# Softmax division of a latent attention by 32x32 squares, a range test on two engines, and two MLP chunks transposed on TensorE

## The chip, the cores and the metric

The kernel runs on one core of one Trainium2 chip. A core has five engines that run their own instruction streams: TensorE (PE, with its weight loads shown apart as PEld), VectorE (DVE), ScalarE (ACT), GpSimd (POOL) and SyncE (SP), which here only issues DMAs. They meet through semaphores. The metric is the device time of one execution in microseconds (us); less is better. Everything is float32.

## The reference

The input is x of 8 batches x 1024 tokens x 256. Two layers are added to it, each on a layer norm of its input:

```
x = x + latent_attention(layernorm(x))
x = x + local_transformer(layernorm(x))

latent_attention(x):                      # 16 heads of 16, rotary part of 32, causal over 1024
    c = x @ W_kv_down                     # 128 wide
    k, v, q = c @ W_k_up, c @ W_v_up, x @ W_q
    k_rope, q_rope = rotary(c @ W_k_rope), rotary(x @ W_q_rope)   # one for all heads
    s = (q . k + q_rope . k_rope) / sqrt(48)
    return (softmax(causal(s)) @ v) @ W_o

local_transformer(x):                     # 2 layers of
    q, k, v = split(shift_token(x) @ wqkv)      # 8 heads of 64
    q, k = xpos(l2norm(q)), xpos(l2norm(k))
    x = x + local_attention(8 q, k, v) @ wo     # windows of 128 with the window before
    h = layernorm(shift_token(x)) * g + b
    a, gate = split(h @ w1 + b1)                # 682 each
    x = x + (a * gelu(gate)) @ w2 + b2
```

## The kernel before

**Latent attention (`mla`, the first 1030 us).** The shared rotary part of the scores is taken out of the softmax as a factor: exp(a + r) = exp(a) x exp(r). `rotary(c, kb)` makes exp(r) for one block of keys kb and one half c of the queries: a matmul into a PSUM bank `psR`, an Exp on ACT into the tile `er` with a sum per row into `most` (L400), a minimum per row on DVE into `least` (L401), and on the diagonal a mask by POOL (L403). At the very end of the stage `most` and `least` are compared with 1e17 and 1e-17; a kernel for the general case runs instead where a value leaves that range. There are 12 such blocks per batch.

A batch is 36 units, one per step. In step s TensorE computes the scores of unit s (four matmuls of 32 rows each side by side, into two pairs of PSUM banks, `scores`, L422), ACT takes their exponentials (two instructions of 128x1024, L430), DVE multiplies the result of the unit before by `er` (`turned`, two instructions, L444), and TensorE multiplies the unit before that with the values (`values`, L455, into `acc`, 32 rows per head: 16 values, and the row sum that a column of ones in v gives). Then the step does what a table, `beside`, gives it: parts of the projections, of the rotary blocks, of the layer norm of the next batches (`statistics`, `normalise`), and of the output of this batch or the one before. Engine orders are written out by hand (`tc.manual_schedule`): the instructions stand on PE, DVE, ACT and POOL in the order in which the Python code makes them; SP's DMAs are ordered by a scheduler. The beside-work shares one pool of two PSUM banks (`psum1`, `bank`), and the scores have two buffers of two banks each.

When four heads (one g of four, for one half c of the queries) are done, `values` has ACT copy `acc` to the tile `oaT` (heads' values in partitions, tokens along the row). One step later `finished(c, g, oT)` divides: four TensorE transposes (`flip`, L203) put tokens into partitions of a bank `pst`, DVE takes the reciprocals of the sums (L472) and multiplies (L473) into `onat`. Later steps turn that back for the output projection: `out_turn(t)`, four transposes of 128x128 into `pso`, which ACT copies to `oT` (L78), and `out_add(t, i)` multiplies by W_o into `psx`, after which DVE adds to x (L500) and SP stores x2d. `value(g)` makes the values; DVE copies them from PSUM (L76). In the last batch, the output work is held back to the end of the stage (`held`). Groups end at steps 14, 15 (c = 1, g = 0, 1), 27, 28 (c = 1, g = 2, 3), 32, 33 (c = 0, g = 0, 1) and 1, 2 of the next batch (c = 0, g = 2, 3), counted by the step that holds their `finished`.

**Local transformer (`local`).** 16 passes (8 batches in layer 0, then 8 in layer 1) of 8 windows, one window per step, software pipelined over 11 steps, again ordered by hand. Each pass needs its input transposed, `xT`, which the generator `stream(b, l)` makes while the pass before runs. It is advanced (`ahead`) at the end of steps i = 3, 4, 5 of that pass, and at two places each, middle and end, of steps 6 and 7. Its parts: loads; in layer 0 the statistics of all 8 blocks; in layer 0 the normalisation of all 8 (L749); then for each half of the tokens the transposition. That is done by `squares`: DVE transposes 32x32 blocks of a tile into the tile `turned` (one buffer, L759), four DMAs write that to DRAM in an order which puts the blocks right (z), and further DMAs read it back as xT, eight per half.

The MLP runs by 32 chunks of 512 tokens (`mlp`): `look_at_chunk`, `norm_chunk` and `turn_chunk` for chunk k + 1 stand inside chunk k's work. `turn_chunk` uses `squares` too (turnedh, zh) and one DMA back into `d`; `scale_chunk` then applies gain and shift on ACT in place (L1034). The first matmuls of the chunk (`up`, ag, L1058) read d, the second ones (psy, L1099 and L1105) are added to x by DVE (L1111). psw (L991) is the output projection of the local attention. The pool `psum` with the tag "mm" has three banks, for pv, s, psw, ag, psy.

## Time and profile before

| What | Value |
|---|---|
| median of 3 runs | 3396.03 us (3395.36 to 3396.98) |
| profiled execution | 3395.82 us |
| its span in the trace | 3393.8 us |
| granted TensorE clock, mean | 0.991 |
| latent attention, one batch in the steady part | 123.02 us |
| one pass of layer 0, of layer 1 | 143.9 us, 142.8 us |
| PE, DVE, ACT, POOL busy share of the span | 97, 79, 49, 39% |

The profiled execution lies 0.2 us under the median. A row of the groups reads: line, engine, operation, tile written and tile read (names of the program), shapes, count | busy time, mean duration in ns | idle time of that engine just before such an instruction, and what ended it. Batch and pass lengths are distances from one to the next of the same instruction in the timeline. In the chain of waits each line is start, length and the work that filled it; x16 says that sixteen instructions are joined.

### The profile page before, as it was taken

How to read it: one execution, taken by the hardware profiler on the slowest of the kernel's cores; microseconds unless marked ns; L12 is line 12 of the kernel's file. 1: busy time of each engine (PE TensorE's matmuls, PEld its weight loads, DVE VectorE, ACT ScalarE, POOL GpSimd, SP SyncE). 2: the span in 40 equal slices, each digit the busy share in tenths (PEclk: the TensorE clock that was granted, in tenths of full speed). 3: DMA queues.
4: the chain of work that ended last, by engine and by line, in shares of the span. 5: the costliest groups of instructions: out<-in, count | busy, mean ns of one | idle time of the engine just before them, and what ended most of it. 6: DMA issues, size and time to landing. Idle time of an engine off the chain costs nothing.

```text
span 3393.8 us, 80114 instructions
## 1 busy us (share of the span) xinstructions
PE 3293.2 (97%) x34194; PEld 1797.8 (53%) x34194; DVE 2682.9 (79%) x4033; ACT 1673.3 (49%) x2046; POOL 1340.0 (39%) x1031
## 2 busy tenths in 40 slices
PE   8999999999997799999999999999999999999998
PEld 2434434443433456566555566565665556665664
DVE  6888988988896777887777887777877778777773
ACT  5777777777762244344444434444444444344441
POOL 1001000000006655555555555555555555555540
PEclk9999999999998899999999999999999999999999
DMA  1000000000032434445445344544545444454332
GB/s 62 8 20 26 8 20 26 8 20 14 14 104 84 128 103 116 120 112 139 111 116 129 109 126 131 144 122 136 133 136 133 126 118 128 128 141 125 107 106 60
DMA packets 370619, 313.87 MB, mean 92 GB/s; under 512 B 154655, under 2 KB 334286, under 8 KB 370126
## 3 DMA queue, kind: packets, MB, share of 16 engines
q1 hardware_dynamic: 368270, 306.26, 33.0%
q8 instruction: 271, 4.44, 0.6%
q10 hardware_dynamic: 1984, 2.41, 0.2%
q14 instruction: 94, 0.77, 0.1%
HBM read 167.00 MB, written 141.56 MB: 91 GB/s over the span
## 4 chain that ended last, share of the span: by engine, by line
PE 86%; DVE 7%; ACT 2%; issue 2%; DMA 1%; POOL 1%; SPq 1%; ACTq 0%; DVEq 0%
PE ag L1058 17%; PE pair L845 11%; PE sc L422 9%; PE acc L455 8%; PE psy L1099 7%; PE psw L991 6%; PE o L958 6%; PE pv L872 6%; PE pair L917 4%; PE psR L200 2%; PE psq L200 2%; PE psx L200 2%; PE s L966 1%; PE pst L203 1%; PE psv L200 1%
## 5 line engine op out<-in xcount | busy, mean ns | idle before, releaser
L444 DVE TENSOR_TENSOR pt<-pt,er 128x1024 f32<-128x1024 f32 x576 | 676.6, 1222 | 6.7 <-ACT pt L430 5.8
L430 ACT ACTIVATE pt<-sc 128x1024 f32<-128x1024 f32 x576 | 559.6, 1024 | 231.9 <-PE sc L422 210.6
L1058 PE MATMUL ag<-d,l 128*128 128x512 f32 x1408 | 646.2, 601 | 28.3 <-ACT d L1034 17.5
L859 POOL TENSOR_TENSOR t<-t,t 128x1024 f32<-128x1024 f32 x128 | 302.4, 2363 | 850.2 <-DVE t L855 850.2
L923 ACT ACT_TABLE_LOAD x120 | 154.0, 1283 | 701.8 <-PE pair L917 701.7
L845 PE MATMUL pair<-l_qkv,xT 128*128 128x512 f32 x1024 | 466.6, 598 | 3.3 <-ACT pt L923 1.3
L1058 PEld LDWEIGHTS ag<-d,l 128*128 128x128 f32 x1408 | 262.5, 191 | 345.5 <-issue 276.1
L125 POOL TENSOR_TENSOR rn<-ss,half 128x16 f32<-128x16 f32 x128 | 373.1, 2915 | 13.7
L422 PE MATMUL sc<-q,k 32*128 32x512 f32 (+3 forms) x3072 | 346.9, 523 | 5.6 <-ACT pt L430 5.5
L845 PEld LDWEIGHTS pair<-l_qkv,xT 128*128 128x128 f32 x1024 | 192.9, 191 | 245.1 <-issue 207.4
L455 PE MATMUL acc<-pt,v 128*32 128x512 f32 (+3 forms) x3072 | 316.3, 497 | 0.4 <-DVE pt L444 0.3
L850 ACT ACTIVATE sq<-pair 128x1024 f32<-128x1024 f32 x128 | 131.1, 1024 | 334.9 <-issue 267.1
L852 DVE TENSOR_TENSOR t<-pair,l_cos 128x1024 f32<-128x1024 f32 x128 | 156.3, 1221 | 160.4 <-ACT sq L850 155.8
L1099 PE MATMUL psy<-l,hid 128*128 128x256 f32 x1280 | 281.5, 379 | 0.0
L1099 PEld LDWEIGHTS psy<-l,hid 128*128 128x128 f32 x1280 | 243.2, 190 | 46.7 <-issue 15.1
L923 ACT ACTIVATE pt<-pair 128x1024 f32<-128x1024 f32 (+1 forms) x256 | 235.0, 968 | 63.2 <-PE pair L917 61.8
L403 POOL TENSOR_SCALAR_AFFINE_SELECT er<-er 128x128 f32<-128x128 f32 x64 | 47.3, 740 | 530.3 <-DVE least L401 530.3
L1071 DVE SCALAR_TENSOR_TENSOR hid<-ag,l_b,ge 128x512 f32<-128x512 f32 x160 | 115.8, 724 | 176.9 <-ACT ge L1070 137.1
L865 POOL TENSOR_TENSOR t<-t,rn 128x1024 f32<-128x1024 f32 x128 | 248.8, 1944 | 10.0
L958 PEld LDWEIGHTS o<-pt,v 128*32 128x32 f32 x7680 | 203.0, 110 | 93.8 <-issue 84.7
L958 PE MATMUL o<-pt,v 128*32 128x128 f32 x7680 | 239.0, 276 | 7.9 <-DVE oT L975 6.6
L991 PE MATMUL psw<-l_o,oT 128*128 128x256 f32 x1024 | 240.2, 388 | 6.2 <-DVE xs L1111 6.2
(131 smaller groups left out, 4790.2 us busy)
## 6 DMA issues: line engine op xcount, KB each, us to landing
z<-turned SPq DMA_DIRECT2D x512, 128.0 KB
qkT<-z SPq DMA_DIRECT2D x128, 512.0 KB
y<-xs SPq DMA_DIRECT2D x128, 128.0 KB
h<-y SPq DMA_DIRECT2D x32, 512.0 KB
zh<-turnedh SPq DMA_DIRECT2D x128, 128.0 KB
d<-zh SPq DMA_DIRECT2D x32, 512.0 KB
zx<-turneds SPq DMA_DIRECT2D x120, 128.0 KB
xT<-zx SPq DMA_DIRECT2D x240, 64.0 KB
```

The costliest lines, as they stand in the source:

```text
L125: nc.gpsimd.tensor_tensor(out_, in_, half[:, :n], ALU.pow)
L422: nc.tensor.matmul(two[n // 2][:, n % 2, lo : lo + w], self.k[g][rows, kb * P : (kb + 1) * P], self.q[rows, g // 2, q0 : q0 + w], start=Tr ...
L430: nc.scalar.activation(pt, sc, AF.Exp, scale=SCALE)
L444: nc.vector.tensor_tensor(t, t, er.to_broadcast([P, 1024 // w, w]), ALU.mult)
L455: nc.tensor.matmul(self.acc[g][32 * n : 32 * n + 32, q0 - c * 512 :], self.v[:, kb, h * VW : h * VW + 32], pts[n // 2][:, n % 2, lo : lo + w],
L845: nc.tensor.matmul(qk[:, n].rearrange("p h d -> p (h d)"), self.left(i)[c], w["qkv"][:, c, n * INNER : (n + 1) * INNER], start=(c == 0), s ...
L859: nc.gpsimd.tensor_tensor(t1, t1, t2, ALU.add)
L923: nc.scalar.activation(pt[:, :, : n * P], flat[:, :, : n * P], AF.Exp, scale=-1.0)
L958: nc.tensor.matmul(o[32 * j : 32 * j + 32, g, a, :], vs[m][:, h * DH + a * 32 : h * DH + a * 32 + 32], pts[m][g][:, place(j), off : off + ...
L991: nc.tensor.matmul(ps[:, i, :], oT[:, c, i * P : (i + 1) * P], self.w["o"][:, c, :], start=(c == 0), stop=(c == 3),)
L1058: nc.tensor.matmul(ps.rearrange("p (s a t) -> p s a t", a=4, t=32), w["1"][:, c, i, :], d.rearrange("p (a s) c t -> p c s a t", a=4)[:, c] ...
L1099: nc.tensor.matmul(ps[:, t, :], hid[:, i, cols], w["2"][:, i, :], start=(t == i == 0), stop=False)
```

## The change

- `finished` no longer uses TensorE. DVE transposes the 32x32 squares of oaT (128x512), takes the reciprocals and multiplies, all in SBUF; two g are packed into one tile of 16 + 16 columns. `turn_back`, one step after every second `finished`, is one more DVE transpose of 128x512 and gives the left operand of `out_add` directly. `out_turn` with its TensorE transposes and ACT copies is gone. The rows of W_o are loaded in the order that the squares leave, by eight DMAs instead of one. `onat` and `oT` are three buffers of 128x512 each.
- `value`: the copy from PSUM goes from DVE to ACT.
- `rotary`: in 6 of the 12 blocks per batch the DVE minimum is replaced by a second Exp on ACT, with the opposite sign, in place in PSUM, summed per row into `inverse`, which is compared with 1e17 at the end.
- `stream`: in layer 0 the statistics of the second half are put beside the normalisation of the first, and the normalisation of the second half comes after the next advance; the squares of both halves come one advance later, at the end of steps 6 and 7 instead of their middle.
- Chunks 0 and 31 of the MLP are transposed by TensorE into a bank of the pool "mm" (eight 128x128 transposes), and ACT applies gain and shift on the way to d; no `squares`, no DMAs. The layout of d is told to `up` through a view.

```diff
-        nc.sync.dma_start(wout, W_o.rearrange("(c p) d -> p c d", p=P))
+        for e in range(2):
+            for r in range(4):
+                lo = 32 * r + HD * e
+                nc.sync.dma_start(
+                    wout[lo : lo + HD],
+                    W_o.rearrange("(m e r p) d -> e r p m d", m=2, e=2, r=4)[e, r],
+                )
...
+        inverse = wp.tile([P, B * 12], F32, name="inverse")
+        nc.gpsimd.memset(least, 1.0)
+        nc.gpsimd.memset(inverse, 1.0)
...
-                on_v(
+                on_a(
                     self.v[:, 2 * g : 2 * g + 2, : NH * VW].rearrange("p a (h d) -> p a h d", h=NH)[..., :HD],
...
                 nc.scalar.activation(er, ps[:, :w], AF.Exp, scale=SCALE, accum_out=most[:, n : n + 1])
-                nc.vector.tensor_reduce(least[:, n : n + 1], er, AX.X, ALU.min)
+                if kb in ((0, 2), (3, 4, 5, 6))[c]:
+                    nc.vector.tensor_reduce(least[:, n : n + 1], er, AX.X, ALU.min)
+                else:
+
+                    nc.scalar.activation(
+                        ps[:, :w], ps[:, :w], AF.Exp, scale=-SCALE, accum_out=inverse[:, n : n + 1]
...
             def finished(self, c, g, oT):
-                ps = bank(f"pst{self.b}_{c}_{g}").rearrange("p (i h d) -> p i h d", i=4, h=4)
-                for i in range(4):
-                    flip(ps[:, i].rearrange("p h d -> p (h d)"), oT[:, i * P : (i + 1) * P])
-                r = self.rs[:, 4 * c : 4 * c + 4, 4 * g : 4 * g + 4]
-                nc.vector.reciprocal(r, ps[:, :, :, HD])
+
+
+                nat = late.tile([P, 16, 32], F32, tag="onat", name=f"onat{self.b}_{c}_{g}", bufs=3)
+                nc.vector.transpose(nat.rearrange("p b d -> p (b d)"), oT)
+                r = self.rs[:, c, g]
+                nc.vector.reciprocal(r, nat[:, :, HD])
+                e = g % 2
+                if e == 0:
+                    self.onat[c, g // 2] = nat
                 nc.vector.tensor_tensor(
-                    self.onat[:, 4 * c : 4 * c + 4, 4 * g : 4 * g + 4, :], ps[:, :, :, :HD],
-                    r.unsqueeze(3).to_broadcast([P, 4, 4, HD]), ALU.mult,
-                )
-
-            def out_turn(self, t):
-                if t == 4:
-                    self.oTs, self.adds = {}, {}
-                elif t == 0:
-                    verdict(self.rs.rearrange("p t h -> p (t h)"), f"a{self.b}")
-                ps = bank(f"pso{self.b}_{t}").rearrange("p (i q) -> p i q", i=4)
-                for i in range(4):
-                    flat = self.onat[:, t + i // 2].rearrange("p h d -> p (h d)")
-                    flip(ps[:, i, :], flat[:, (i % 2) * P : (i % 2 + 1) * P])
-                self.oTs[t] = late.tile([P, 4, P], F32, tag="oT", name=f"oT{self.b}_{t}", bufs=2)
-                on_a(self.oTs[t], ps)
+                    self.onat[c, g // 2][:, :, HD * e : HD * e + HD], nat[:, :, :HD],
+                    r.unsqueeze(2).to_broadcast([P, 16, HD]), ALU.mult,
+                )
+
+            def turn_back(self, c, g):
+                if g % 2:
+                    t = late.tile([P, 512], F32, tag="oT", name=f"oT{self.b}_{c}_{g}", bufs=3)
+                    nc.vector.transpose(t, self.onat.pop((c, g // 2)).rearrange("p b d -> p (b d)"))
+                    self.oTs[c, g // 2] = t
+                if (c, g) == (0, 3):
+                    verdict(self.rs.rearrange("p c g b -> p (c g b)"), f"a{self.b}")
 
             def out_add(self, t, i, c=None):
 
@@ -493,9 +508,10 @@
                     self.adds[t] = bank(f"psx{self.b}_{t}").rearrange("p (i d) -> p i d", i=2)
                 ps = self.adds[t]
                 for n in range(2) if c is None else (c,):
-                    times(ps[:, i], self.oTs[t][:, 2 * i + n, :], wout[:, n, :], n == 0, n == 1)
+                    col = (t + i) % 4 * P
+                    times(ps[:, i], self.oTs[t // 4, n][:, col : col + P], wout[:, n, :], n == 0, n == 1)
                 if i == 1 and c != 0:
-                    del self.oTs[t], self.adds[t]
+                    del self.adds[t]
...
-            (5, 0, "query", 0, 0, 1), (5, -1, "out_turn", 0), (5, 1, "normalise", 0, 1),
-            (6, -1, "out_add", 0, 0), (6, -1, "out_turn", 2), (6, 1, "normalise", 1, 0),
+            (5, 0, "query", 0, 0, 1), (5, 1, "normalise", 0, 1),
+            (6, -1, "out_add", 0, 0), (6, 1, "normalise", 1, 0),
-            (30, 1, "rotary", 1, 3), (30, 0, "out_turn", 4),
+            (30, 1, "rotary", 1, 3),
-            (34, 1, "rotary", 1, 5), (34, 0, "out_turn", 6), (34, 2, "statistics", 1, 0),
+            (34, 1, "rotary", 1, 5), (34, 2, "statistics", 1, 0),
...
-                        for act, args in held[:3]:
+                        for act, args in held[:2]:
                             act(*args)
                     ended = []
                     if len(line) > 2 or b == B and line:
                         bt, unit, pts = line.pop(0)
                         ended = [(bt, e) for e in bt.values(unit, pts)]
                     if b == B and step == 0:
-                        for act, args in held[3:]:
+                        for act, args in held[2:]:
                             act(*args)
                     do(b, step)
+                    if turning:
+                        bt, e = turning.pop(0)
+                        bt.turn_back(*e)
                     if done:
                         bt, e = done.pop(0)
                         bt.finished(*e)
+                        turning.append((bt, e[:2]))
...
+        nc.vector.tensor_scalar(ok[:, 2, :], inverse, TURN, None, ALU.is_le)
...
             if l == 0:
-                found = [statistics(xs_[:, part], f"s{b}_{n}") for n, part in enumerate(parts)]
+                found = [statistics(xs_[:, parts[0]], f"s{b}_0")]
             yield
             if l == 0:
-                for part, f in zip(parts, found):
-                    normalise(xs_[:, part], f)
+                normalise(xs_[:, parts[0]], found[0])
+                found.append(statistics(xs_[:, parts[1]], f"s{b}_1"))
             yield
             xT = pxT.tile([P, 2, T + 1], F32, tag="xT", name=f"xT{b}_{l}")
             nc.gpsimd.memset(xT[:, 1, 0:1], 0.0)
             for n in range(NCH):
+                if l == 0 and n == ((l, b) == (0, 0)):
+                    normalise(xs_[:, parts[1]], found[1])
                 if (l, b) == (0, 0):
                     for c in range(2):
                         turn(xT, 1 + n * CH, xs_[:, parts[n]], f"s{b}_{l}_{n}", chunks=(c,))
                         yield xs_, xT
                     continue
+                yield xs_, xT
                 z = zxs[n]
                 squares(xs_[:, parts[n]], f"s{b}_{l}_{n}", z)
...
                yield xs_, xT
-                yield xs_, xT
...
+        ON_PE = (0, len(chunks) - 1)
+
         def turn_chunk(k):
 
-            if k < len(chunks):
+            if k < len(chunks) and k not in ON_PE:
                 n, m = chunks[k]
                 z = zhs[k % 2]
                 squares(made[n].hs.pop(m), f"h{made[n].key(m)}", z)
@@ -1029,12 +1055,25 @@
                 nc.sync.dma_start(ds[k].rearrange("p b c t -> p (b c t)"), z.rearrange("p a f -> p (a f)"))
 
         def scale_chunk(k, w):
-            if k < len(chunks):
+            if k in ON_PE:
+                n, m = chunks[k]
+                d = p2.tile([P, 2, CH], F32, tag="d", name=f"d{made[n].key(m)}")
+                t = made[n].hs.pop(m)
+                for c in range(2):
+                    ps = psum.tile([P, CH], F32, tag="mm", name=f"psth{k}_{c}")
+                    for i in range(ST):
+                        nc.tensor.transpose(ps[:, i * P : (i + 1) * P], t[:, i, c * P : (c + 1) * P], ident)
+                    nc.scalar.activation(
+                        d[:, c], ps, AF.Identity, scale=w["gain"][:, c : c + 1], bias=w["shift"][:, c : c + 1]
+                    )
+                ds[k] = d.rearrange("p c (s a t) -> p c s a t", a=4, t=32)
+            elif k < len(chunks):
                 for c in range(2):
                     nc.scalar.activation(
                         ds[k][:, :, c], ds[k][:, :, c], AF.Identity, scale=w["gain"][:, c : c + 1],
                         bias=w["shift"][:, c : c + 1],
                     )
+                ds[k] = ds[k].rearrange("p (a s) c t -> p c s a t", a=4)
 
         def mlp():
 
@@ -1057,7 +1096,7 @@
                     for c in range(2):
                         nc.tensor.matmul(
                             ps.rearrange("p (s a t) -> p s a t", a=4, t=32), w["1"][:, c, i, :],
-                            d.rearrange("p (a s) c t -> p c s a t", a=4)[:, c],
+                            d[:, c],
                             start=(c == 0), stop=(c == 1),
                         )
                     return ps
```

More of the change, by code (lines that the diff above doesn't have):

```diff
@@ L409, in start @@
                 b = self.b
-                self.onat = late.tile([P, NT, NH, HD], F32, tag="onat", name=f"onat{b}")
-                self.rs = small.tile([P, NT, NH], F32, tag="rs", name=f"rs{b}")
-                self.acc = {}
+                self.rs = small.tile([P, 2, 4, 16], F32, tag="rs", name=f"rs{b}")
+                self.acc, self.onat, self.oTs, self.adds = {}, {}, {}, {}
             def scores(self, key, parts):
@@ L576, in mla @@
         E = mybir.EngineType
-        line, done = [], []
+        line, done, turning = [], [], []
         with tc.manual_schedule(engines={E.PE, E.DVE, E.Activation, E.Pool}):
@@ L605, in mla @@
                         bt.finished(*e)
+                        turning.append((bt, e[:2]))
                     done += ended
-        ok = small.tile([P, 2, B * 12], F32, tag="okr", name="okr", bufs=1)
+        ok = small.tile([P, 3, B * 12], F32, tag="okr", name="okr", bufs=1)
         nc.vector.tensor_scalar(ok[:, 0, :], most, TURN, None, ALU.is_le)
         nc.vector.tensor_scalar(ok[:, 1, :], least, 1 / TURN, None, ALU.is_ge)
+        nc.vector.tensor_scalar(ok[:, 2, :], inverse, TURN, None, ALU.is_le)
         verdict.add(ok.rearrange("p m n -> p (m n)"), "turn")
```

## The prediction

> **What bounds the kernel now.** I read four views, in this order: busy time by engine, busy time by stretch of time, the groups of instructions with what ended the idle time before them, and the chain of waits in three places. The page and the stretches (in the stretches each pair is length, then PE, PEld, DVE, ACT, POOL busy, the granted TensorE clock, the DMA share and GB/s):
>
> ```profile
> PE 3293.2 (97%) x34194; PEld 1797.8 (53%) x34194; DVE 2682.9 (79%) x4033; ACT 1673.3 (49%) x2046; POOL 1340.0 (39%) x1031
> ```
> ```profile
> 380.00:500.00 120.00, 118.99 (x1312) 47.74 (x1308) 106.20 (x140) 88.76 (x123) 7.96 (x10) 1.00 0.06 19
> 1035.00:1100.00 65.00, 49.14 (x461) 23.72 (x459) 48.97 (x76) 17.31 (x20) 52.38 (x32) 0.87 0.31 88
> 1100.00:1300.00 200.00, 177.94 (x1998) 106.47 (x1999) 158.58 (x257) 68.80 (x75) 117.15 (x85) 0.94 0.44 114
> 1300.00:1800.00 500.00, 494.49 (x5105) 302.42 (x5104) 395.00 (x662) 205.15 (x223) 274.95 (x205) 1.00 0.44 119
> 3300.00:3394.00 94.00, 77.69 (x470) 48.96 (x468) 35.20 (x70) 13.65 (x19) 2.23 (x3) 0.94 0.22 63
> ```
>
> The average says TensorE. The stretches say: TensorE in the latent attention (99% in 380 to 500, where DVE is at 88%) and in the passes, but neither in the fill of the second stage (1035 to 1180) nor in the tail (after 3348). So each part of the change is priced in its own stretch.
>
> ```profile
> L444 DVE TENSOR_TENSOR pt<-pt,er 128x1024 f32<-128x1024 f32 x576 | 676.6, 1222 | 6.7 <-ACT pt L430 5.8
> L430 ACT ACTIVATE pt<-sc 128x1024 f32<-128x1024 f32 x576 | 559.6, 1024 | 231.9 <-PE sc L422 210.6 <-issue 10.6 <-DMA l_cos<-in_xpos_cos_dram 4.1
> L991 PE MATMUL psw<-l_o,oT 128*128 128x256 f32 x1024 | 240.2, 388 | 6.2 <-DVE xs L1111 6.2
> L885 DVE STREAM_TRANSPOSE turned<-t 128x512 f32<-128x512 f32 x256 | 165.4, 681 | 4.1 <-POOL t L865 4.0
> L203 PE MATMUL pst<-ident,oaT 128*128 128x128 f32 x256 | 42.0, 287 | 3.5 <-ACT er L400 3.4 <-ACT oaT L78 0.2
> L401 DVE TENSOR_REDUCE least<-er 128x1 f32<-128x512 f32 x48 | 32.6, 682 | 29.7 <-ACT er L400 29.7
> L473 DVE TENSOR_TENSOR onat<-pst,rs 128x256 f32<-128x256 f32 x64 | 27.2, 425 | 2.2
> L76 DVE COPY v<-psv 128x512 f32<-128x512 f32 x32 | 22.2, 692 | 18.6 <-PE psv L200 17.9
> L203 PE MATMUL pso<-ident,onat 128*128 128x128 f32 x128 | 21.1, 286 | 0.7 <-DVE onat L473 0.7
> ```
>
> TensorE's idle time here is small in every group (the last columns): its 36 steps per batch are full of its own work. But a step has a second length. In the chain of batch 3, where TensorE has least beside the attention (steps 24 to 26):
>
> ```profile
> 492.61 1.18 PE sc L422 x13
> 495.66 1.18 PE sc L422 x8
> 498.70 1.18 PE sc L422 x8
> ```
>
> These scores start 3.05 and 3.04 us apart and take 1.18, not the 1.07 of other steps: they wait for the second exponential (L430, .92 from start to start) to free their PSUM. So about 3.07 us is the floor of a step, whatever TensorE is spared. The other two places:
>
> ```profile
> 1176.07 3.20 DMA d<-zh
> 1180.16 5.97 PE ag L1058 x8
> ```
> ```profile
> 3350.99 3.88 DMA d<-zh
> 3355.76 20.77 PE ag L1058 x44
> ```
>
> The first and the last MLP chunk come late through a DMA; TensorE is idle 8.97 us before the first (from 1171.2) and 7.61 before the last (from 3348.15).
>
> **The change part by part.** The profiled execution took 3395.82 us, of which 3393.8 is the span; the median of the runs is 3396.03, so the sum is made against 3396. What the page cannot tell, 0.2% or 7 us, I count as no change. Distances "from start to start" are from the timeline; they are less than the durations because instructions of one engine overlap.
>
> *1. Division in squares, per batch.* Removed from TensorE: 12 groups of four transposes (pst 8, pso 4). A group takes .58 start to start: 12 x .58 = 7.0 us per batch. From ACT: 4 copies oT (587 ns, .50). The new DVE work has no row of its own shape; the nearest is L885, the same instruction on the same 128x512 (681 ns, .61 start to start). Eight transposes in `finished` and four in `turn_back`: 12 x .61 = 7.3 us. Reciprocal (.25) and product (.34) stay; from SBUF instead of PSUM I take them as equal (bounds: -.1 to +.2 each).
>
> What TensorE gets from it goes by step. Lengths before, and what is left after .58 is taken, but not under 3.07: steps 1, 2, 6, 32 and 33 (3.52 each) give .45 each; 5 gives .39, 14 (3.30) .23, 15 (4.01) .58, 30 (3.86) .35, 34 (3.31) .24; 27 gives .15, because its exponentials already start .4 late behind the two masked copies of k; 28 nothing, for part 2 fills its ACT. That is 4.2 of the 7.0.
>
> *2. Range test shared, values copied by ACT, per batch.* DVE loses six `least` (.47 + .19 + 3 x .60 + .19 = 2.65) and four copies v (L76, 4 x .61 = 2.43). ACT gets four copies (nearest row: L78, .50 to .59) and six exponentials with a sum (a 512 wide one 608 ns, its read of the sum 210; net .59, so 2.3 + .6 = 2.9), less the oT copies: +2.9 of some 91 in 123, and spread; each of these steps has .9 to 1.4 us of ACT left, except 28 (.20), already counted. The inverse also holds its PSUM bank .6 longer; with pst and pso gone the two banks have room.
>
> DVE's sum is +7.3 - 2.65 - 2.43 = +2.2 us on 108.9 in a batch (106.20 of 120, times 123.0): not an average limit (111 of 121). Where it falls matters. The removed work lies in steps 2, 9, 14, 15, 24, 25 and 27 to 29, the added in 1 to 3, 14 to 16, 27 to 29 and 32 to 34. A step costs DVE 2.27 for its two products (L444, 1.135 start to start). Steps 32 to 34 come to 2.27 + .6 (sum into x) + 1.2; 2.27 + .6 (least) + 1.2; 2.27 + .47 + .8 (statistics) + .6 = about 12.2 us against 3 x 3.07 = 9.2. The products may run 1.4 us later than now before `values`, two steps on, waits for them. So 1.6 to 1.9 of stall there, and in steps 1 to 3 about .6 by the same reckoning: 2.4 (0 if DVE starts these steps early; 4.5 if the new instructions cost half as much again). Net per batch -4.2 + 2.4 = -1.8, for batches 1 to 6 -11. Batch 0 and the prologue, where ACT and psR alternate and ACT gets four inverses and two copies: +2 (.5 to 4). Batch 7 is bound by DVE after 985, and the end of the stage loses a TensorE round trip of 1.5 us: +2 together. Sum of the latent attention: -7, between -22 (no stall) and +15.
>
> At this place a rule speaks against the change. The row: a 128x512 transpose on DVE has 681 ns, four 128x128 ones on TensorE .58 us. The Trainium skill, "VectorE: DVE Perf Modes", section "Rules for kernel authors", tells authors to put a 128x128 transpose on TensorE where PSUM will do as its destination, and the section "The three transpose paths" gives 311 ns for 128x128 in 32x32 blocks on VectorE (bf16). An estimate by that page would be 4 x .311 = 1.24 per transpose, 14.9 per batch, and 7.6 more of DVE time than by the row; were all of it stall, 8 x 7.6 = 61 us slower. The row has the shape and type, so the row stands.
>
> W_o in eight DMAs instead of one: SP issues them in the prologue (.45 each by the z issues, 3.2 more), wanted first in step 31; the cover is 100 us. The memsets are POOL's, idle there. The third range check, on 96 columns, lies after the stage: under .5.
>
> *3. The streams, layer 0.* In the fill, squares of the two halves of xT stand next to each other and the second waits for the first one's DMA (`turned` has one buffer): DVE idles 3.79 (to 1111.30) and 4.15 (to 1127.55). In the whole trace:
>
> ```profile
> DVE turneds L759 <- DMA z<-turned: 91.6, 26, 7.4
> ```
>
> Half a step apart, the first goes; the second largely comes back, as the eight xT transfers are queued on SP ahead of the next. I take 3 (0 to 7). In the six steady layer-0 passes DVE is busy without a gap from the statistics (1356.67) through the eight normalisations (2.63) to L1111 (1388.76), and TensorE waits 1.03 for it. Half of both, 1.3 us, moves behind L1111: the wait goes, and what is late next is unseen, so -.75 x 6 = -4.5 (-6.2 to -1). In the other passes the 91.6 is covered (TensorE has 142.2 of 144), and that squares and xT transfers go out half a step (9 us) later on DVE and SP costs nothing as long as the transfers end before the next pass's first qk, for which some 20 us are left now; without that cover up to 9 a pass.
>
> *4. Chunks 0 and 31.* Removed: turnedh (4 x .35), four DMAs zh, one d and its issue. Chunk 0: h is ready at 1170.88; after it eight transposes (2 x .58) and ACT (.69), so ag at about 1172.8 instead of 1180.16: -7.4. But DVE works through most of that gap (8.26 of 8.9), and `hid` and the sums wait for it, so not all of it lasts: I take -6 (-9 to -2). Together with 3 the fill gives -9. Chunk 31: h is ready at 3342.3, psth0 runs at 3348.1, psth1 when L1111 (3348.06 to 3348.75) has freed its bank, ACT .69 after: ag at 3350.1, -5.6 (-7 to -3).
>
> The clock: after both gaps the granted clock is half for 5 to 7 us (the first four or five ag average 1093 and 1057 ns instead of 592). The Trainium skill, "TensorE: Matmul & The Clock Gate", section "Part 1: The HAM clock gate", has the half clock begin after about 3.4 us without work; a gap of 2 us would then keep full speed and give another estimated 1 to 2 us at each. I leave it out of the sum.
>
> Sum: -7 - 9 - 4.5 - 5.6 = -26: 3370 us.
>
> **The rivals.**
> *A, DVE keeps up.* DVE ends the products .8 to 3 us early in all steps but 28, which speaks for it; 32 to 34 against. Then 4.2 per batch: 2.4 x 6 = 14 less, 3356.
> *B, the attention gives nothing.* Stalls of 4.2 per batch cancel TensorE's gain (88% DVE busy now; the added work comes in threes). With the ends' 19 and +4 for batches 0 and 7: 3381.
> *C, slower.* DVE sets the pace where heads end: if all 7.3 us of transposes come out as stall, less 4.2: +3.1 x 7 = 22, +4, less the ends: 3403. It decides from 6.3 us of stall per batch on (net 2.1 x 7 + 4 = 19). Against: the 5.1 us removed and slack of about 2 us before most steps.
> *D, the second stage's waits were hidden anyway.* DVE has 49 of 65 us in the fill, and POOL 52; if something else follows, 3 and 4 give only chunk 31 and 3 us: 3396 - 7 - 8.6 = 3380.
>
> **How the numbers follow.** Forecast 3370 (3360 to 3378) .50; A .14; B .15; D .11; C .10. The range leaves out C and the far end of A: 3351 to 3389. Faster by over 0.2% (under 3389): .50 + .14 + .13 + .09 = .86; the same .05 from the weak ends of B and D, slower .09.
>
> **What would show it.** Batch period 123.0 before: 121.2 expected, 118.8 under A, 123 under B, over 126 under C. Steps 1, 2, 6 near 3.07. "acc <- DVE pt" waits of TensorE near steps 35 and 0: absent under A. Chunk 0: TensorE idle under 3 us near 1170. Tail: 2 us between psbad and ag. The psw wait of 6.2 gone. Wrong would make it a DVE transpose much over .68 from these layouts, or ACT late in steps 24 to 30, with exponentials starting after 1.2 us.

## The result and the profile after

The changed kernel takes 3352.9 us (median of 4, 3352.46 to 3355.65) against 3395.8 for the kernel before (4 runs): a ratio of 0.9875, with a 95% interval of 0.9858 to 0.9892. The profiled execution has a span of 3350.7 us against 3393.8, 43.1 less. Where those come from is read by following the same instruction through both timelines: how much earlier does it start? The difference between two marks is what the stretch between them gave.

| Stretch, from mark to mark | predicted | measured |
|---|---|---|
| start to batch 1 of the attention | +2 | -1.4 |
| batches 1 to 6 | -11 (-1.8 each) | -6.6 (-1.10 each) |
| batch 7 to the first qk of the second stage | +2 | +2.7 |
| fill, first qk to first psy | -9 | -13.8 |
| six layer-0 passes, psy of chunk 0 to psy of chunk 12 | -4.5 | -12.3 (-2.04 each) |
| the rest of the passes, to psy of chunk 30 | 0 | -5.3 (-.94 in each layer-1 pass, +1.15 at the change of layers) |
| tail, psy of chunk 30 to the end | -5.6 | -6.4 |
| sum | -26 | -43.1 |

Two of these rows are no clear gain or loss. From batch 7 to the first qk it takes 132.8 us in the kernel before, but 136.2 in e1 (below), which leaves the code of the attention as it is; and the pass with the change of layers takes 145.7 before and 146.8 after, but 146.4 in e4, which leaves that place as it is. So the +2.7 and most of the +1.15 lie within what runs show without an edit there.

First the busy times of the whole execution and of the stretches, kernel after (columns as before: PE, PEld, DVE, ACT, POOL, granted clock, DMA share, GB/s):

```profile
PE 3272.6 (98%) x33826; PEld 1778.5 (53%) x33826; DVE 2711.0 (81%) x4042; ACT 1692.5 (51%) x2142; POOL 1340.9 (40%) x1033
```
```profile
380.00:500.00 120.00, 118.81 (x1286) 46.34 (x1282) 108.91 (x141) 92.39 (x136) 9.16 (x10) 1.00 0.06 19
...
1094.00:1285.00 191.00, 181.61 (x2009) 108.86 (x2009) 164.06 (x267) 72.32 (x79) 120.69 (x89) 0.96 0.44 116
1285.00:1780.00 495.00, 494.55 (x5105) 302.53 (x5104) 400.69 (x661) 207.09 (x224) 279.71 (x205) 1.00 0.45 121
...
3255.00:3350.00 95.00, 85.38 (x586) 55.30 (x578) 39.34 (x79) 20.16 (x25) 5.64 (x8) 0.97 0.17 52
```

VectorE has 108.91 of 120 us in the attention (before 106.20), ScalarE 92.39 (88.76). Scaled to a batch that is 1.8 and 2.9 more, where the prediction had 2.2 and 2.9. TensorE now idles .45 us in the 495 of the layer-0 passes, where it idled 5.5 in 500 (three and a half passes in each case): some 1.5 of the 2.04 us that each pass gained. Next, groups of the kernel after:

```profile
L459 DVE TENSOR_TENSOR pt<-pt,er 128x1024 f32<-128x1024 f32 x576 | 676.2, 1220 | 32.1 <-ACT pt L445 31.7
L486 DVE STREAM_TRANSPOSE onat<-oaT 128x512 f32<-128x512 f32 x64 | 44.9, 702 | 0.0
L500 DVE STREAM_TRANSPOSE oT<-onat 128x512 f32<-128x512 f32 x32 | 22.3, 698 | 0.0
L1014 PE MATMUL psw<-l_o,oT 128*128 128x256 f32 x1024 | 240.8, 389 | 0.0
```

The new DVE transposes take 702 and 698 ns; the row from which I priced them had 681. (The estimate of 1.24 us, worked out from the 311 ns that the Trainium skill, "VectorE: DVE Perf Modes", "The three transpose paths", gives for 128x128 in bf16, does not hold for these; the measurement decides.) The psw wait of 6.2 us is gone, as predicted. Of the waits of the kernel before, two that change (engine, what waits, for what: total, times, longest):

```profile
PEld acc L455 <- DVE pt L444: 40.9, 56, 1.5
PE ag L1058 <- ACT v L78: 8.8, 13, 0.7
```

and in the kernel after:

```profile
PEld acc L470 <- DVE pt L459: 105.9, 144, 2.1
DVE turneds L780 <- DMA z<-turned: 10.9, 8, 4.5
PE acc L470 <- DVE pt L459: 8.8, 23, 1.3
```

TensorE now waits for VectorE's products: a little of it shows as idle PE (8.8 us, before .3), more in the weight loads that wait (40.9 to 105.9). The wait for `turned`, 91.6 before, has all but gone, and with it a wait that I had not priced: ag behind the copy of v no longer appears at all. Chain of waits after, in batch 3, in the fill and in the tail:

```profile
516.34 2.27 DVE pt L459 x2
520.57 2.28 DVE pt L459 x2
```
```profile
1162.53 0.69 ACT d L1066
1163.27 3.70 PE ag L1097 x8
```
```profile
3312.10 0.66 PE psth L1065 x4
...
3312.88 19.08 PE ag L1097 x44
```

The products of VectorE that are issued in steps 33 and 34 of a batch are now on the chain. The first eight ag take 3.70 us instead of 5.97, and the 44 of the last chunk 19.08 instead of 20.77: TensorE idles only .48 us before the first ag and .19 before psth of the last chunk, and the clock stays at 1.00 (windows 1163 to 1176 and 3308 to 3316). This agrees with the Trainium skill ("TensorE: Matmul & The Clock Gate", "Part 1: The HAM clock gate"), which has the half clock begin after about 3.4 us without work.

### The profile page after: what moved, and what is told of

It is laid out like the page before. It is cut to its first block, busy times and chain, and to the rows that moved or that the text cites. A ratio compares the mean times of both kernels' runs of the same rounds, so it can differ in the third digit from the quotient of the medians.

```text
span 3350.7 us, 79434 instructions
## 1 busy us (share of the span) xinstructions
PE 3272.6 (98%) x33826; PEld 1778.5 (53%) x33826; DVE 2711.0 (81%) x4042; ACT 1692.5 (51%) x2142; POOL 1340.9 (40%) x1033
## 4 chain that ended last, share of the span: by engine, by line
PE 88%; DVE 5%; ACT 2%; issue 1%; DMA 1%; SPq 1%; POOL 1%; ACTq 0%; DVEq 0%
PE ag L1097 17%; PE pair L868 13%; PE sc L437 9%; PE psy L1138 8%; PE acc L470 7%; PE psw L1014 7%; PE o L981 6%; PE pv L895 6%; PE pair L940 4%; DVE pt L459 2%; PE psx L200 2%; PE psq L200 2%; PE s L989 2%; PE psR L200 1%; PE psy L1144 1%
## 5 line engine op out<-in xcount | busy, mean ns | idle before, releaser
L437 PE MATMUL sc<-q,k 32*128 32x512 f32 (+3 forms) x3072 | 368.9, 522 | 6.5 <-ACT pt L445 6.4
L470 PE MATMUL acc<-pt,v 128*32 128x512 f32 (+3 forms) x3072 | 336.1, 497 | 9.1 <-DVE pt L459 8.8
L437 PEld LDWEIGHTS sc<-q,k 32*128 32x128 f32 x3072 | 157.9, 184 | 199.6 <-ACT pt L445 149.3
```

The lines of the kernel that those rows point to most:

```text
L437: nc.tensor.matmul(two[n // 2][:, n % 2, lo : lo + w], self.k[g][rows, kb * P : (kb + 1) * P], self.q[rows, g // 2, q0 : q0 + w], start=Tr ...
L470: nc.tensor.matmul(self.acc[g][32 * n : 32 * n + 32, q0 - c * 512 :], self.v[:, kb, h * VW : h * VW + 32], pts[n // 2][:, n % 2, lo : lo + w],
```

## Experiments

Two theories stand for the second stage. S: the wait of VectorE for the one tile `turned` cost TensorE .9 us in every pass, through what was queued behind it. H, my prediction: that wait was covered. For the attention, M: VectorE's new work stalls TensorE in the steps where heads end; and later W: the stall comes from a wait at the head of VectorE's queue, with other work behind it. Against them stand "VectorE keeps up" (A, as in the prediction) and "VectorE's amount of work counts" (B here, another than the B of the prediction).

### The streams alone, both edits, and the squares alone

```diff
  e1_streams: the two hunks of `stream` from the change
  e2_squares_later: only
+                yield xs_, xT
                 z = zxs[n]
                 squares(xs_[:, parts[n]], f"s{b}_{l}_{n}", z)
...
-                yield xs_, xT
```

> The kernel before with both edits of the streams alone (squares half a step later, statistics and normalisation spread). Theory S: in every pass DVE stood behind the squares' wait for the one tile `turned`, so the reciprocal of the sums and hid came late, a bank came free late and TensorE lost .9 us (the ag wait of .68); in layer 0 the psw wait of 1.03 goes as well. Then a layer-0 pass takes 141.9 instead of 143.9 us, a layer-1 pass 141.9 instead of 142.8, the transition gives about 1 back and the fill 1 to 4: 3374 to 3378 us. Rival H, the prediction's view (the waits were covered, only the psw wait goes): layer-0 passes 143.1, layer-1 passes unchanged at 142.8, 3388 us.

> The kernel before with the squares half a step later and nothing else. Theory S: layer-1 passes 141.9, layer-0 passes 142.9 (the psw wait of 6.2 us in all stays), the ag wait behind the copy of v is gone, total wait of DVE for z falls from 91.6 to under 20: 3379 to 3383 us. Rival H2, the spreading of the statistics is what made room: layer-0 passes stay at 143.9, only layer 1 can gain: 3389 us or more.

Measured: e1 3376.66 us, ratio 0.9946 (0.9929 to 0.9963); e2 3381.24, ratio 0.9957 (0.9940 to 0.9973). A layer-0 pass took 143.9 before, 141.9 in e1, 143.0 in e2; a layer-1 pass 142.8, 141.9, 141.9. So the squares' place gives .94 in every pass of both layers, and the spreading of the normalisation the other 1.1 in layer 0 (in e2 the psw wait of 6.2 us is still there). S holds, H falls. The fill of e1 is 2.9 us shorter from the first qk to the first psy, but its first qk came 3.4 later, so e1 does not show a gain in the fill.

### What the wait did, and taking it away without moving anything

The same place of a layer-1 pass in the timeline, before: VectorE, then TensorE (start, length, what, idle before and its end):

```profile
2415.20 1.42 DVE L759 STREAM_TRANSPOSE turneds<-xs 128x256 f32<-128x256 f32 x4 [4.04 <-DMA z<-turned]
2416.55 1.72 DVE L970 RECIPROCAL rs<-s 128x256 f32<-128x256 f32 x1
...
2419.39 0.74 DVE L1071 SCALAR_TENSOR_TENSOR hid<-ag,l_b,ge 128x512 f32<-128x512 f32 x1
```
```profile
2421.47 2.84 PE L1058 MATMUL ag<-d,l 128*128 128x512 f32 x6 [0.68 <-ACT v L78]
```

and after:

```profile
2379.87 1.74 DVE L993 RECIPROCAL rs<-s 128x256 f32<-128x256 f32 x1
...
2385.66 0.75 DVE L1110 SCALAR_TENSOR_TENSOR hid<-ag,l_b,ge 128x512 f32<-128x512 f32 x1 [2.86 <-ACT ge L1109]
2386.36 1.43 DVE L780 STREAM_TRANSPOSE turneds<-xs 128x256 f32<-128x256 f32 x4
```
```profile
2389.41 3.60 PE L1097 MATMUL ag<-d,l 128*128 128x512 f32 x8
```

Before, the squares stood at the head of VectorE's queue for 4.04 us until the DMAs had read `turned`, which the transposes of q and k had just filled. The reciprocal that frees the bank of s, and hid, which frees the banks of ag, waited behind it; by this reading the three banks of the pool "mm" ran out, and ag started .68 late. The profile names the copy of v, because that came last. After, the reciprocal runs first and the squares find `turned` free. To tell the wait from the place:

```diff
-                squares(xs_[:, parts[n]], f"s{b}_{l}_{n}", z)
+                squares(xs_[:, parts[n]], f"s{b}_{l}_{n}", z, "turned" if l else "x2")
```

(`squares` takes the tile's tag as a new argument; in layer 0 the tile of load_x2 is not in use.)

> The kernel before with its engine orders unchanged, only that in layer 0 the squares of the streams use another tile than the one that the transposes of q and k use (the tile of load_x2, which layer 0 does not need). That takes away what makes them wait, not their place. Theory S (the wait is the cause): layer-0 passes 142.9 instead of 143.9, layer 1 as before (142.8), ag waits behind v in layer 1 alone, fill 1 to 7 us shorter: 3383 to 3389 us. Rival H3 (their place is the cause: 1.4 us of transposes ahead of the reciprocal): layer-0 passes stay at 143.9, 3392 to 3396 us.

Measured: 3388.95 us, ratio 0.9976 (0.9966 to 0.9986). Layer-0 passes 143.0, layer-1 passes unchanged. The waits of e3:

```profile
DVE turneds L759 <- DMA z<-turned: 41.1, 13, 7.7
PE psw L991 <- DVE xs L1111: 6.1, 6, 1.0
PE ag L1058 <- ACT v L78: 4.7, 7, 0.7
```

With the orders of PE, DVE, ACT and POOL as before, another tile alone gives the .94 in the six layer-0 passes, which have it, and of the 13 waits of ag the 6 in layer 0 are gone: there the single buffer is the cause, not the place of the squares. For layer 1, which kept the one tile, e2 shows the same gain from the later place. The fill gave 1.2 us, at the low end of what was expected.

### The two chunks alone

The hunks of `turn_chunk`, `scale_chunk` and `up` on the kernel before.

> The kernel before with chunks 0 and 31 on TensorE and nothing else. If the saved half clock counts in full: first ag at 1172 to 1173 instead of 1180.16 and 2.3 us less after it, tail 7.9 shorter: 3378 to 3380 us. Rival, the prediction's terms (DVE holds back part of the fill, half clock left out): 6 and 5.6 us: 3384 us.

Measured: 3381.05 us, ratio 0.9953 (0.9937 to 0.9970). The fill gave 9.4 (first qk to first psy), the tail 7.7; 1.3 us were lost before chunk 30, where ag waited 2.2 us for its d. That wait is .9 in the kernel before and 2.0 in e6, whose second stage is that of the kernel before, so it moves from run to run without this edit; it puts e4 just above the 3378 to 3380 us that were expected. The chain of e4 in the tail shows the full speed:

```profile
3342.52 0.66 PE psth L1042 x4
...
3343.30 19.08 PE ag L1074 x44
```

So the saved half clock has to be counted: from the first qk, the first ag came 7.1 us earlier, close to the 7.4 of the direct path, and the eight ag took 2.3 less, together the 9.4. VectorE held back next to nothing of it.

### The attention: division alone, sharing alone

```diff
  e5_division: the change's `finished`, `turn_back`, `out_add`, W_o; `rotary` and `value` as before
  e6_shared: the change's `rotary` and `value`; division as before
```

> The kernel before with the division in squares alone: VectorE keeps all minima and the copies of v. Theory M (VectorE stalls TensorE where heads end): TensorE's steps get 4 to 5.6 us per batch shorter, but VectorE, with 7.3 more and nothing less, falls behind in steps 27 to 29 too, where its products had .3 to 1.1 us to spare before; a batch takes 122.5 to 124.5 us, 3392 to 3404 us. Rival A (VectorE keeps up, the saved transposes count in full): a batch 118.8, 3362 to 3368 us.

> The kernel before with six minima replaced by ScalarE's second exponential and the copies of v on ScalarE, and nothing else. Theory M: TensorE sets the pace of the steps, so 5.1 us less on VectorE buys nothing by itself, and ScalarE is late in steps 15, 16 and 28 to 31: a batch 123.0 to 124, 3396 to 3404 us; with the division alone it does not add up to the whole change, which gives 1.10 per batch. Rival: VectorE was the bound of the attention: a batch under 122, under 3390 us.

Measured: e5 3416.48 us, ratio 1.0059 (1.0042 to 1.0076), a batch 125.69; e6 3398.46, ratio 1.0009 (0.9999 to 1.0018), a batch 123.00. Together they give 121.92. A falls: alone, the division costs more than even M expected. Batch 3 by groups of steps (us, steps 8 to 13 and 18 to 26 are 21.1 and 29.0 in all of them):

| | batch | 0-7 | 14-17 | 27-31 | 32-35 |
|---|---|---|---|---|---|
| before | 123.02 | 27.50 | 14.18 | 17.56 | 13.72 |
| after | 121.92 | 27.38 | 13.30 | 17.21 | 13.97 |
| e5 division alone | 125.69 | 27.98 | 14.45 | 19.18 | 14.02 |
| e6 sharing alone | 123.00 | 27.50 | 14.46 | 17.27 | 13.72 |
| e11 division alone, minima later | 122.91 | 28.67 | 12.89 | 17.07 | 14.21 |
| e7 after, evened out | 120.15 | 25.60 | 13.30 | 17.21 | 13.97 |
| e8 e7, exchanged | 122.73 | 25.61 | 14.45 | 19.18 | 13.44 |
| e9 e7, minima later | 120.08 | 26.15 | 13.30 | 17.19 | 13.38 |
| e10 e9, exchanged | 118.19 | 25.61 | 12.89 | 16.19 | 13.44 |
| e12 e10, divisions later | 117.68 | 25.73 | 12.89 | 16.19 | 12.81 |

A group of four transposes less should take .58 from each of steps 14 and 15; e5 gets longer in 14 to 17. The timeline of its VectorE around the minimum of step 14:

```profile
457.92 1.31 DVE L450 TENSOR_TENSOR pt<-pt,er 128x1024 f32<-128x1024 f32 x1
459.37 0.42 DVE L408 TENSOR_REDUCE least<-er 128x1 f32<-128x256 f32 x1
459.70 4.86 DVE L450 TENSOR_TENSOR pt<-pt,er 128x1024 f32<-128x1024 f32 x4
467.44 0.55 DVE L408 TENSOR_REDUCE least<-er 128x1 f32<-128x384 f32 x1 [2.88 <-ACT er L407]
467.91 0.70 DVE L477 STREAM_TRANSPOSE onat<-oaT 128x512 f32<-128x512 f32 x1
```

VectorE stands idle for 2.88 us with a minimum at its head that needs an `er` which ScalarE makes only after this step's exponentials; the division and the products are behind it. The kernel before had that wait too (2.87), but without a stall behind it: by this reading its shorter division, without the transposes, fitted into the slack that was left. The next run tests that.

### The same work in another order

Theory W: sharing the range test helped because it took such waits away (in steps 14 and 27), not because it took work away. Undo the sharing, keep all the work, and take the wait away by order alone:

```diff
-                nc.vector.tensor_reduce(least[:, n : n + 1], er, AX.X, ALU.min)
-                if q0 == kb * P:
-                    nc.gpsimd.affine_select(...)
+                minima.append((least[:, n : n + 1], er, q0 == kb * P))
...
+                    take_minima()
                     do(b, step)
```

`take_minima` issues the minima, and the masks behind them, that the step before has put into the list.

> As e5 (division in squares alone, all twelve minima and the value copies on VectorE), with all minima one step later in VectorE's order. The amount of VectorE's work is that of e5. Theory W: what made e5 slower is the wait of VectorE for er in steps 14 (2.88 us) and 27 (1.23) with divisions and products behind it; without it steps 14 to 17 and 27 to 31 recover 2 to 3 us: a batch 122.5 to 124.0 instead of 125.70, 3391 to 3404 us. Rival B (the busy time counts): 125.4 to 125.9, 3413 to 3418 us.

Measured: 3396.01 us, ratio 0.9995 (0.9985 to 1.0004), a batch 122.91; steps 14 to 17 and 27 to 31 recovered 1.56 and 2.11, more than expected, and .9 was lost again in 0 to 7 and 32 to 35, into which minima now fall. With the same work a batch is 2.8 us shorter: for the loss in those two groups W holds, and B, which expected 125.4 or more, falls. VectorE of e11 in step 14, where the minimum (L283) now finds its `er` made:

```profile
456.99 2.35 DVE L460 TENSOR_TENSOR pt<-pt,er 128x1024 f32<-128x1024 f32 x2
459.26 0.55 DVE L283 TENSOR_REDUCE least<-er 128x1 f32<-128x384 f32 x1
459.72 0.70 DVE L487 STREAM_TRANSPOSE onat<-oaT 128x512 f32<-128x512 f32 x1
```

Waits of e5, then of e11:

```profile
DVE least L408 <- ACT er L407: 47.6, 26, 2.9
PE acc L461 <- DVE pt L450: 16.3, 44, 1.4
```
```profile
PE acc L471 <- DVE pt L460: 8.1, 21, 1.8
DVE least L283 <- ACT er L422: 3.4, 2, 2.0
```

### The rest of the loss in the attention

e7 evens VectorE's work out; e8 puts six minima back and takes the second exponential where ScalarE has room; e9 is e7 with the minima one step later, and e10 is that with e8's exchange, except that kb = 3 has the exponential too.

```diff
  e7_statistics, on the changed kernel:
-            (3, 0, "keys", 1, 0), (3, 0, "keys", 1, 1, 0), (3, 1, "statistics", 1, 1),
+            (3, 0, "keys", 1, 0), (3, 0, "keys", 1, 1, 0),
-            (24, 1, "value", 0),
-            (25, 1, "value", 1),
-            (26, 1, "keys", 0, 1), (26, 2, "statistics", 0, 1),
+            (24, 1, "value", 0), (24, 2, "statistics", 0, 1),
+            (25, 1, "value", 1), (25, 2, "statistics", 1, 0),
+            (26, 1, "keys", 0, 1), (26, 2, "statistics", 1, 1),
-            (34, 1, "rotary", 1, 5), (34, 2, "statistics", 1, 0),
+            (34, 1, "rotary", 1, 5),
...
+                        if e[:2] == (0, 1):
+                            turning.append((bt, None))
  e8_swap, on e7:
-                if kb in ((0, 2), (3, 4, 5, 6))[c]:
+                if (c, kb) not in ((1, 4), (1, 5)):
  e9_later_minima, on e7: `minima` as in e11
  e10_later_minima_swap, on e9:
+                if (c, kb) not in ((1, 3), (1, 4), (1, 5)):
```

> The changed kernel with VectorE's work evened out: the statistics of the second half of the next input moved from steps 34 and 3 to 24 to 26, and the turning back of the squares of c = 0, g = 0 and 1 one step later (35 instead of 34). Theory M: the 4.6 us per batch that steps 0, 5, 7, 16, 29, 31 and 35 have lost come mostly from VectorE's crowding in 32 to 34 and 1 to 3; with 1.4 us less there and .99 less in step 3 a batch takes 119.5 to 120.7 instead of 121.92: 3336 to 3345 us. Rival: ScalarE's late exponentials (steps 28 to 31, 35) make that loss: within 2 us of the changed kernel, 3351 to 3355 us.

> As e7, and the second exponential only in the blocks of steps 33 and 34 (c = 1, kb = 4, 5); the other ten blocks go back to VectorE's minimum, in steps where its products have over 2 us to spare. ScalarE's exponentials are then no longer late in steps 15, 28, 29 and 30 (starting 1.18 after the step instead of 1.57 to 1.99). Theory M with ScalarE's part: 1 us per batch better than e7, 118.5 to 119.8, 3328 to 3338 us. Rival (VectorE has no room in 27 to 31): slower than e7.

> As e7, and each minimum that VectorE still takes (with the mask behind it) stands one step later in its order, behind the next two products instead of ahead of them, so that VectorE never waits for ScalarE's er at its head. Theory W (the loss left in steps 29 to 35 begins with that wait: 1.93 us idle before the minimum in step 30, after which the products run late into 33): a batch 118.6 to 119.5 instead of 120.15, 3328 to 3337 us. Rival (the amount of VectorE's work in 32 and 33 makes the stall, whatever came before): 120.0 to 120.3, within 2 us of e7.

> As e9, and the second exponential only in c = 1, kb = 3, 4, 5; the other nine blocks have VectorE's minimum, one step later. It is e8's exchange without the wait at VectorE's head. Theory W: e8 was slow (122.74) because the minima put back in steps 14 and 27 waited 2.87 and 2.30 us for er with the divisions and products behind them; without that wait the exchange helps, since ScalarE is no longer late in 15, 16 and 28 to 30 and VectorE has less in 33: 118.0 to 119.2, 3325 to 3335 us, not slower than e9. Rival B (VectorE's busy time is what counts, 1.4 us more per batch than e9): 121 or more, 3347 us or more.

Measured: e7 3341.04 us, ratio 0.9842 (0.9826 to 0.9859); e8 3362.69, 0.9901 (0.9885 to 0.9918); e9 3340.79, 0.9830 (0.9813 to 0.9846); e10 3326.95, 0.9788 (0.9772 to 0.9805).

e7 came in as expected, but in another place: steps 0 to 7 got 1.8 shorter, 32 to 35 not at all. What stalls step 35 is queued ahead of what e7 took out of 34. (e7 makes two edits at once, the statistics and the turning back; their shares are not told apart.) e8 was a miss: it lengthens just the two groups that e5 had lengthened, to the same hundredths, by putting back the waits:

```profile
DVE least L412 <- ACT er L410: 65.5, 26, 7.6
```

e9 was a miss too: 120.08 us lies in the range of its rival, 120.0 to 120.3, so here order alone bought nothing in sum. In steps 32 to 35 it gave .6, less than I had claimed, and it lost as much in 0 to 7, where minima and sums now come later: VectorE waits at its head for psx instead, 19.8 us in all instead of 9.4 in e7. But e10 shows what the order was good for: the exchange that cost e8 2.6 us a batch against e7 gains 1.9 against e9. Of the 4.5 us between e8 and e10, 1.6 lie in steps 14 to 17, which kb = 3 does not touch; of the 3.0 in steps 27 to 31 the part that kb = 3 has is not shown.

At last e12 takes the two crowded divisions apart:

```diff
+                    if done and done[0] is None:
+                        done.pop(0)
-                    if done:
+                    elif done:
...
+                    if ended and ended[0][1][:2] == (0, 0):
+                        done.append(None)
                     done += ended
```

> As e10, and the divisions of c = 0, g = 0 and 1 each one step later (33 and 34 instead of 32 and 33; their turning back in step 0 of the next batch). In e10 VectorE has 2.2 us beside its products in step 32 and 1.3 in 33, its products of 32 and 33 end .16 and .29 us ahead of the matmuls that wait for them, and step 35 takes 4.29 us instead of 3.38; in 34 VectorE has nothing. Theory W: spread over 32 to 34, the delay in 35 goes down to .3 or less: a batch 117.3 to 117.7 instead of 118.2, 3319 to 3325 us. Rival (TensorE's own psx in 35 makes its length): a batch 118.0 to 118.4, 3325 to 3330 us.

Measured: 3323.3 us (median of 5), ratio 0.9786 (0.9773 to 0.9800), a batch 117.68; steps 32 to 35 12.81. The time came in as expected, but step 35 still takes 4.00, where .3 or less over 3.38 was expected. What is left there is no wait for VectorE: TensorE does not idle in this step, its acc and psx take 1.00 and 1.29 as in the kernel before, but its scores take 1.70 instead of 1.08, while ScalarE, whose exponentials free the scores' PSUM, works without a gap from 504.4 to 510.5. Waits of e12:

```profile
DVE least L286 <- ACT er L425: 9.9, 2, 7.6
PE acc L481 <- DVE pt L470: 4.3, 9, 1.3
```

e12 has the lowest time of all that ran; its interval lies clear of the changed kernel's (0.9858 to 0.9892), but not of that of e10.

## Why the prediction was right or wrong

The time lay in the range, but only just (3352.9, where the range began at 3351), and outside the 3360 to 3378 that was given half of the chance. The direction was right; the sum was 17 us short, and the terms tell why.

**The streams (part 3): wrong, the largest miss (17.6 against 4.5 after the fill).** The failing step is "In the other passes the 91.6 is covered (TensorE has 142.2 of 144)". It was not covered: the .7 of ag that was left in each pass, named after the copy of v, was the trace of it. I had priced the wait only where VectorE itself was the bound, and had not asked who stood behind the squares in VectorE's queue. The psw term was right: it went, 1.1 per layer-0 pass, though I took .75. Rival D, hidden anyway, fell with it.

**Chunks 0 and 31 (part 4): mechanism right, size low.** Fill 13.8 against 9, tail 6.4 against 5.6; e4 alone gave 9.4 and 7.7. The missing term is the half clock that I had named and left out: 2.3 us on the first eight ag and 1.7 on the last 44. That VectorE would hold back the fill, which I took 1.4 off for, did not show. The other 4.4 us of the fill came with the rest of the change, where the prediction had 3 for the streams; no run shows which part gave them. In the tail the last chunk's ag came 6.2 us earlier, .6 more than the 5.6, and the 2 us foreseen between psbad and ag did not appear. Some 1.4 of the tail's gain went again in the end, where the last store lands 9.0 us after the last psy instead of 7.55; that span lies between 7.4 and 9.0 in the runs, and its cause is open.

**Division in squares (part 1): right in kind, wrong in two sizes.** The shorter steps gave 5.65 per batch instead of 4.2, because 3.07 is no floor of a single step: step 14 went to 2.72 and others to 2.93, with the next scores a little longer. The kernel before had shown as much, for its step 23 takes 2.93. (By its own rule the sum should also have had .58 for step 30, not .35.) The longer ones took back 4.56 instead of 2.4: 35 and 0 (+1.51, +.81) for the 1.8 foreseen behind steps 32 to 34, 5 and 7 (+.39, +.23) for the .6 foreseen behind 1 to 3, and 16, 29 and 31 (+.41, +.53, +.68), which I had not listed. There ScalarE is late: they stay at 3.91, 3.71 and 4.04 in e9, and in e10, which is e9 with ScalarE relieved, they are 3.51, 3.15 and 3.58 long. Net 1.10 instead of 1.8 per batch. The prologue and batch 0, where I feared +2, gained 1.4.

**Range test and copies (part 2): right effect, wrong reason for most of it.** I credited 5.1 us of work taken from VectorE. e11 shows that with all that work still there a batch takes 122.91 instead of 125.69 as soon as the minima stand behind the products: 2.8 of the 3.8 us by which the sharing shortens a batch with the division (125.69 to 121.92). In steps 14 to 17 and 27 to 31, where heads end, order alone recovers all that the sharing did; there it bought the removal of waits at VectorE's head in steps 14 and 27. The other 1.0 us is not split further. And order is not all: e10, with the minima as late as in e11 but less and better spread work on VectorE, is 4.7 us a batch shorter still. I had shown the row (29.7 us of idle VectorE before `least`, ended by er) and did not ask what stood behind it: the same mistake as with the streams.

**The rivals.** A's total of 3356 lies nearest to the result, by luck: A is wrong, for a batch takes 121.92, not 118.8, and the gain that it put there came in the second stage. C's mechanism (transposes come out as stall) is what e5 shows when the division stands alone: 2.7 us per batch slower. That the whole change did not go this way is due to the sharing, without which (e5) a batch takes 125.69.

## What to carry to other kernels

On an engine that works in order, price a wait by what is queued behind it and how much time that has to spare, not by whether the engine is busy on average. A tile with one buffer that two steps share, or a test on data that another engine makes late, costs nothing where it stands last and a stall where it stands first; another tile (e3), or one place later in the order (e11), can take it away without taking work away, though e9 shows that the later place may cost elsewhere what it gains. And a total that agrees with a rival says little: compare the two timelines mark by mark before believing its mechanism.

## What the runs showed that I had not expected

- Two edits that are worthless or harmful alone (division 1.0059, sharing 1.0009) are worth 1.1 us per batch together; a later place of the minima (e11, 122.91) clears most of the same room for the division.
- In the changed kernel the second exponential, in place in PSUM, took 645 ns for 512 columns and its read of the sum 229, where er into SBUF took 624 and 222. In the kernel before, er took 608 and 210.
- A gap of TensorE of .2 to .5 us left its clock at 1.00, gaps of 7.6 and 9 us were followed by four to six slower matmuls, most of them of 1061 ns instead of 592 (by eight of them in e3, after a gap of 8.2 us).
